# The clustering stage of an attention-and-clustering block: a reordered search, squares on GpSimd, queries projected elsewhere, roots with a bias, and filling in other places

## The chip, the core and the metric

The kernel runs on one core of a Trainium2 chip. The core has a tensor engine (TensorE, PE in the profile, with its weight loads shown apart as PEld), a vector engine (VectorE, DVE), a scalar engine (ScalarE, ACT), a general engine (GpSimd, POOL), and a sync engine (SyncE, SP) that issues most of the transfers. Each engine works through its own list of instructions in order and waits on semaphores for the others. The metric is the time of one execution on the device, in microseconds (us).

## What is computed

The input is four images of 256 channels and 64 x 64 pixels, in float32. Layer 0 is self-attention over the 4096 pixels of an image. Layer 1 normalizes over the whole image, clusters the pixels, projects, and goes through a perceptron and two batch norms. The change touches the clustering and the projections of the next image's attention:

```python
q = einsum('oc,bcn->bno', wq, xf) + bq          # 32 channels
k = einsum('oc,bcn->bon', wk, xf) + bk
attn = softmax(einsum('bnd,bdm->bnm', q, k))
v = einsum('oc,bcn->bon', wv, xf) + bv          # 256 channels
x = gamma[0] * einsum('bcn,bmn->bcm', v, attn) + x
...
feat, val = conv1x1(xn, f_w, f_b), conv1x1(xn, v_w, v_b)   # xn = group_norm(x); 96 channels each
# 4 heads of 24 channels, 2 x 2 folds of the image, 2 x 2 centres in each fold
cn = cen * rsqrt((cen * cen).sum(-1) + 1e-12)
pn = pts * rsqrt((pts * pts).sum(-1) + 1e-12)
sim = sigmoid(beta + alpha * einsum('bmc,bnc->bmn', cn, pn))
mask = one_hot(argmax(sim, axis=1))              # the best of 4 centres for every pixel and head
sim = sim * mask
agg = (einsum('bmn,bnc->bmc', sim, v2) + v_cen) / (mask.sum(-1) + 1.0)
out = einsum('bmn,bmc->bnc', sim, agg)
y = x + ls1 * conv1x1(out, proj_w, proj_b)
```

## The kernel before

The four images go one after the other. For each, `weighting` runs the attention: 8 blocks of 512 queries by 8 groups of 512 keys, 64 units in all. Then `cluster` runs the clustering and `mlp` the perceptron and the pointwise layer. The order of the instructions is written out by hand: an engine does them in the order in which the program emits them, and the text below says "emitted" for that.

**Filling.** Attention of the next image needs its v, its keys and its queries, projected from x. `parts.projections` (L1105) is a list of 36 closures: 32 of `v_half`, each for 128 pixels (two matmuls of 128 x 256 in float32, which the profile counts as four; every second one is followed by a ScalarE copy of a pair, L434), and four of `halved` (keys and queries, each for half of the image: matmuls at L344, a ScalarE op at L361 for the high half, a VectorE op at L362 for the low half, and four transfers to DRAM on SP). `fill(n)` takes the next n of the list and emits them. It is called at many places between the end of `weighting` and the start of the perceptron, where TensorE would wait for a vector chain. Images 0, 1 and 2 have the next image's projections as filling; the last image has `late_block`, the rest of the perceptron of the image before.

**End of `weighting`** (L1061 to L1098). The softmax sums of the last query block are reduced on VectorE (L730, L732), summed over partitions by TensorE (L1070), inverted on VectorE (L1079), sent to all partitions by TensorE (L1085) and copied by ScalarE (L1092). Then the last block is scaled (L1095), added to x (L828) and its statistics taken (`seen`, L832; `pooled`, L837). The block before it is brought back by a transfer that adds to x, `back_one` (L815), issued on GpSimd's queue two units before the end.

**`group_norm`** (L296) makes mean and variance over the whole image with three tiny matmuls (L302, L303, L313), a root on ScalarE and a reciprocal on VectorE (`rsqrt`, L216: add, root, reciprocal). `gn1` is that ahead of the clustering, `gn2` that ahead of the perceptron.

**`cluster`**: centres (`pcen`, L1145), their norms (`len`, L1184), then a loop over 8 pixel blocks (L1281) in which TensorE makes f and v and the products with the centres in one matmul (L1293), VectorE moves them out of PSUM (L1302, L1309), and `heads` squares f (L1273: on GpSimd, for the last block on VectorE) and sums the squares by head (L1274). The image is in two halves, f = 0 (blocks 0 to 3) and f = 1. `similar(f)` (L1227) turns the squares into 1/norm (root and reciprocal), multiplies, and takes tanh on ScalarE; `affine(f)` turns tanh into the sigmoid; `largest(f)` (L1240) finds the best of four centres in five VectorE ops (maximum, is_equal, product with a rank, maximum, is_equal); `weights(f)` masks; `count(f)` counts. `summed` (L1323) then aggregates on TensorE in two passes, first the pooled v, then the weighted v. Counts (L1352), transposes (L1363, L1372), the scaled aggregate (L1376) and its projection `gp` (L1384) follow, and `products` (L1406) spreads the result back over the pixels with the second statistics on VectorE (L1418, L1399). At its end the first three units of the next image's scores are made (`score`, L471; copies at L484; the key loads are issued on SP, L449).

`turn()` makes sums of the perceptron's weights on GpSimd: `turn_mlp` (L246, L247; for the last image it is emitted at L1065 instead) and `turn_w2` (L1577, L1579, L1581). It is emitted after `similar(1)`, so on GpSimd's list it stands right behind the squares of block 6.

The order at the search, whose lines the prediction follows:

```python
        fill(4 if nxt else 2)
        heads(NBLK - 1)
        similar(1)
        fill(0 if nxt else 2)
        summed(lambda j, q: pool_w[:, j], True)
        gelu(1)
        turn()
        fill(8 if nxt else 4)
        table(AF.Sqrt)

        affine(0)
        largest(0)
        affine(1)
        largest(1)
```

Of the kernel before, what the change touches and what calls it, by code (L numbers as in the profile page):

```python
# [14 lines left out]
P = 128  # L15
B, C, H, W = 4, 256, 64, 64
N = H * W
# [43 lines left out]
def attention_then_cluster_block(  # L61
# [153 lines left out]

    def rsqrt(dst, src, eps, meanwhile=lambda: None):  # L216

        nc.vector.tensor_scalar(dst, src, eps, None, ALU.add)
        nc.scalar.activation(dst, dst, AF.Sqrt)
        meanwhile()  # L220
        nc.vector.reciprocal(dst, dst)
# [74 lines left out]
    def group_norm(b, which, stats, fill, between=lambda: None, meanwhile=lambda: None):  # L296
# [19 lines left out]
        fill(3 if which == "gn1" else 2)  # L316
# [14 lines left out]
    def attention(b, xs, ys):  # L331
# [87 lines left out]
        def v_half(i):  # L419
            if i == 0:  # L420
                own["v"] = big.tile([P, N // P, C], F32, tag="v", name=f"v_{b}")
            if i % 2 == 0:
                vps[0] = ps_m.tile([P, 2, C], F32, tag="m", name=f"vp_{b}_{i // 2}")
            o = (i * P) % XT
            for k in range(KC):
                nc.tensor.matmul(  # L426
                    vps[0][:, i % 2, :],
                    xs[i * P // XT][:, k, o : o + P],
                    wv_s[:, k, :],
                    start=(k == 0),  # L430
                    stop=(k == KC - 1),
                )
            if i % 2:
                nc.scalar.copy(own["v"][:, i - 1 : i + 1, :], vps[0])  # L434

        def v_pair(i):
            v_half(2 * i)
            v_half(2 * i + 1)
# [497 lines left out]
        def weighting(next_x, fill, early, begin):  # L936
# [129 lines left out]
            table(AF.Sqrt)  # L1066
            two = ps_s.tile([P, 2, NB], F32, tag="s", name=f"den_{b}_{nb}")
# [9 lines left out]
            fill(2)  # L1077
# [4 lines left out]
            seen(nb - 1)  # L1082
# [10 lines left out]
            fill(6)  # L1093
# [11 lines left out]
        parts.projections = [lambda i=i: v_half(i) for i in range(N // P)]  # L1105
        parts.projections[14:14] = [lambda: halved("q", 0)]
        parts.projections[13:13] = [lambda: halved("k", 0)]
        parts.projections += [lambda: halved("k", 1), lambda: halved("q", 1)]
# [5 lines left out]
    def cluster(b, ys, stats, cells, rest, fill, gelu, nxt, maxima, turn):  # L1114
# [8 lines left out]
        ga, gb = group_norm(b, "gn1", stats, fill, rest, pooling)  # L1123
# [103 lines left out]
        def similar(f):  # L1227

            sg = sgs[f]
            rsqrt(prns[f], prns[f], L2_EPS, lambda: table(AF.Gelu_apprx_tanh))  # L1230
# [9 lines left out]
        def largest(f):  # L1240

            sg, o, best = sgs[f], oh[:, f * 256 : (f + 1) * 256], bests[f]
            nc.vector.tensor_reduce(best, quad(sg), AX.X, ALU.max)
            nc.vector.tensor_tensor(quad(o), quad(sg), over_m(best), ALU.is_equal)
            nc.vector.tensor_tensor(
# [3 lines left out]
            nc.vector.tensor_tensor(quad(o), quad(o), over_m(best), ALU.is_equal)  # L1249

# [858 lines left out]
```

## Time and profile before

The times of three runs are 3134.9, 3135.86 and 3136.3 us; the median is 3135.86 us. The profiled execution took 3135.99 us. Its span, from the first to the last instruction of the program that was recorded, is 3134.2 us. The mean granted clock of TensorE is 0.993.

The clustering stage of image 0, in stretches (times from the start of the span; the columns are microseconds busy on each engine, from the view that sums over windows):

| stretch of image 0 | from - to | length | PE | DVE | ACT | POOL |
|---|---|---|---|---|---|---|
| end of weighting to gn1 | 528.90 - 539.30 | 10.40 | 8.84 | 10.32 | 4.75 | 2.49 |
| gn1 to the first f and v product | 539.30 - 547.90 | 8.60 | 8.47 | 5.95 | 3.18 | 0.00 |
| f and v products | 547.90 - 570.60 | 22.70 | 22.70 | 13.31 | 13.14 | 5.94 |
| to the second aggregation | 570.60 - 584.25 | 13.65 | 13.39 | 10.97 | 6.33 | 6.84 |
| aggregation to the spread | 584.25 - 589.00 | 4.75 | 3.86 | 2.38 | 3.55 | 0.00 |
| spread, statistics, scores, to gn2 | 589.00 - 605.75 | 16.75 | 13.76 | 15.44 | 10.70 | 11.97 |
| gn2 and the start of the perceptron | 605.75 - 613.90 | 8.15 | 6.96 | 5.24 | 4.15 | 3.00 |

The other three images have the same stage from 1299, 2071 and 2818 us on. In the timeline, a row is an instruction (or several alike, "x4"): its start and its duration in us, engine, source line, operation, tile written and tiles read, shape, and in brackets how long the engine was idle before it and what it had been waiting for. A duration runs from when the instruction starts on its engine, so a stand inside it counts as busy. Matmul ends are modelled. In rows of windows the columns are: the window, its length, then busy us and number of instructions of PE, PEld, DVE, ACT and POOL, then the granted TensorE clock, the share of the DMA engines and GB/s.

### The profile page before, as it was taken

How to read it: one execution, taken by the hardware profiler on the slowest of the kernel's cores; microseconds unless marked ns; L12 is line 12 of the kernel's file. 1: busy time of each engine (PE TensorE's matmuls, PEld its weight loads, DVE VectorE, ACT ScalarE, POOL GpSimd, SP SyncE). 2: the span in 40 equal slices, each digit the busy share in tenths (PEclk: the TensorE clock that was granted, in tenths of full speed). 3: DMA queues.
4: the chain of work that ended last, by engine and by line, in shares of the span. 5: the costliest groups of instructions: out<-in, count | busy, mean ns of one | idle time of the engine just before them, and what ended most of it. 6: DMA issues, size and time to landing. Idle time of an engine off the chain costs nothing.

```text
span 3134.2 us, 41370 instructions
## 1 busy us (share of the span) xinstructions
PE 3053.2 (97%) x14210; PEld 2498.2 (80%) x14210; DVE 2514.4 (80%) x3574; ACT 1778.9 (57%) x2817; POOL 2324.7 (74%) x2232
## 2 busy tenths in 40 slices
PE   7999999999999999999999999999999999998999
PEld 5788887788688888878868888886877888875886
DVE  4999888777798888877779888877768988887675
ACT  4666664544566666454456666645446666655344
POOL 5888887477588888647758888955766988893563
PEclk9999999999999999999999999999999999999999
DMA  5112226200112123510011222431011112160000
GB/s 167 45 61 64 61 61 186 71 17 28 48 47 68 55 61 100 154 58 18 28 51 51 65 63 65 113 125 58 28 41 44 59 57 67 54 153 1 14 21 28
DMA packets 105570, 200.40 MB, mean 64 GB/s; under 512 B 14880, under 2 KB 30864, under 8 KB 103824
## 3 DMA queue, kind: packets, MB, share of 16 engines
q1 hardware_dynamic: 100464, 178.66, 18.2%
q0 software_dynamic: 4256, 18.90, 2.9%
q8 instruction: 113, 1.85, 0.2%
q14 instruction: 97, 0.79, 0.1%
q10 hardware_dynamic: 640, 0.20, 0.0%
HBM read 147.01 MB, written 48.34 MB: 62 GB/s over the span
## 4 chain that ended last, share of the span: by engine, by line
PE 74%; DVE 10%; POOL 8%; issue 3%; ACT 3%; DMA 2%; SPq 1%; ACTq 0%; POOLq 0%; DVEq 0%
PE av L716 35%; PE mo L1721 10%; PE sc L471 7%; PE hq L1804 5%; PE hp L1804 3%; PE hr L1804 3%; PE fv L1293 3%; POOL acc L646 2%; DVE top L495 2%; DVE s L637 2%; POOL t L646 2%; POOL s L646 1%; PE mo L1705 1%; DMA w<-in_w 1%; PE vp L426 1%
## 5 line engine op out<-in xcount | busy, mean ns | idle before, releaser
L484 ACT COPY s<-sc 128x1024 f32<-128x1024 f32 x512 | 515.2, 1012 | 433.8 <-PE sc L471 426.3
L637 DVE TENSOR_TENSOR s<-s,hold 128x1024 f32<-128x1024 f32 x512 | 598.6, 1209 | 6.7 <-ACT hold L620 5.0
L646 POOL TENSOR_TENSOR acc<-acc,t 128x512 f32<-128x512 f32 x408 | 541.4, 1347 | 0.0
L716 PE MATMUL av<-s,sum 128*128 128x256 f32 x2048 | 526.9, 380 | 3.7 <-POOL s L646 3.5
L716 PE MATMUL av<-t,v 128*128 128x256 f32 x2048 | 528.0, 380 | 2.5 <-POOL t L646 2.2
L716 PE MATMUL av<-s,v 128*128 128x256 f32 x2048 | 526.7, 380 | 2.1 <-ACT xn L1672 1.1
L646 POOL TENSOR_TENSOR s<-t,s 128x512 f32<-128x512 f32 x256 | 340.5, 1330 | 224.8 <-DVE t L660 157.5
L660 DVE TENSOR_TENSOR t<-s,hold 128x1024 f32<-128x1024 f32 x256 | 311.8, 1218 | 186.6 <-POOL acc L646 95.5
L495 DVE TENSOR_TENSOR top<-sc,top 128x1024 f32<-128x1024 f32 x350 | 426.8, 1219 | 31.4 <-ACT s L484 28.0
L716 PEld LDWEIGHTS av<-s,v 128*128 128x128 f32 x2048 | 387.6, 190 | 64.9 <-ACT xn L1672 2.3
L716 PEld LDWEIGHTS av<-t,v 128*128 128x128 f32 x2048 | 387.9, 190 | 63.2 <-POOL t L646 8.5
L716 PEld LDWEIGHTS av<-s,sum 128*128 128x128 f32 x2048 | 388.1, 190 | 61.3 <-POOL s L646 8.5
L1759 ACT ACTIVATE hs<-hs,pv_s 128x256 f32<-128x256 f32 x496 | 232.5, 502 | 352.6 <-DVE hs L1795 352.6
L471 PE MATMUL sc<-q,k 128*128 128x512 f32 x1024 | 394.2, 469 | 24.8 <-ACT s L484 9.5
L1721 PE MATMUL mo<-hs,w 128*128 128x256 f32 x1512 | 384.8, 381 | 0.0
L646 POOL TENSOR_TENSOR t<-s 128x512 f32<-128x512 f32 x256 | 330.7, 1292 | 46.8 <-PE av L716 33.4
L1721 PEld LDWEIGHTS mo<-hs,w 128*128 128x128 f32 x1512 | 283.8, 190 | 46.8 <-ACT hs L1759 6.2
L641 ACT ACTIVATE hold<-s 128x512 f32<-128x512 f32 x256 | 154.2, 602 | 212.5 <-DVE s L637 210.7
L1795 DVE TENSOR_TENSOR hs<-hq,hs 128x256 f32<-128x256 f32 x496 | 198.7, 421 | 85.9 <-PE hq L1804 75.9
L643 ACT ACTIVATE s<-s 128x1024 f32<-128x1024 f32 x256 | 266.9, 1043 | 0.0
L471 PEld LDWEIGHTS sc<-q,k 128*128 128x128 f32 x1024 | 175.5, 191 | 113.7 <-DVE top L495 54.2
L716 PE MATMUL av<-t,sum 128*128 128x256 f32 x1024 | 262.4, 378 | 0.0
(296 smaller groups left out, 4871.3 us busy)
## 6 DMA issues: line engine op xcount, KB each, us to landing
k<-k SPq DMA_DIRECT2D x248, 256.0 KB, 2.7
x<-in_x SPq DMA_DIRECT2D x62, 512.0 KB, 6.8
out<-xn SPq DMA_DIRECT2D x62, 256.0 KB, 2.1
att<-t SPq DMA_DIRECT2D x56, 256.0 KB, 4.0
x<-att POOLq DMA_DIRECT2D x12, 1024.0 KB, 10.0
w<-in_w SPq DMA_DIRECT2D x8, 1024.0 KB, 12.0
q<-q SPq DMA_DIRECT2D x31, 256.0 KB, 4.0
rden<-row_rd SPq DMA_DIRECT2D x28, 256.0 KB, 3.6
```

Of the source, the lines that this page charges most:

```text
L471: nc.tensor.matmul(sc[:, r, :], k_s[:, (2 * h + r) * P : (2 * h + r + 1) * P], qs[u // GRP], start=True, stop=True,)
L484: nc.scalar.copy(slots[u][:, PAIR[h]].rearrange("p h r n -> p r h n"), tiles(sc))
L495: nc.vector.tensor_tensor(top, src, top if saved[nb] is None else saved[nb], ALU.max)
L637: nc.vector.tensor_tensor(sh, sh, mb.to_broadcast([P, 2, 2, QW]), ALU.subtract)
L643: nc.scalar.activation(s[:, PAIR[1]], s[:, PAIR[1]], AF.Exp)
L646: nc.gpsimd.tensor_tensor(out, x, y, op)
L660: nc.vector.tensor_tensor(t31[u], s[:, B11 : B22 + 1 : 2], b12.to_broadcast([P, 2, 2, QW]), ALU.add)
L716: nc.tensor.matmul(av[bank][:, half_ * QW : (half_ + 1) * QW], a[:, r], t[:, r], start=(g == 0 and r == 0 and i in (1, 7, 2, 4)), stop=(g ...
L1721: return nc.tensor.matmul(bank[:, half * HB : (half + 1) * HB], a[:, j], t, start=start, stop=stop)
L1759: nc.scalar.activation(src, src, AF.Gelu_apprx_tanh, bias=pvc("b1", P, j + 4 * (i > 1)))
L1795: nc.vector.tensor_tensor(dst, ps, term, ALU.add)
L1804: nc.tensor.matmul(out, w, x, start=True, stop=True)
```

## The change

It does six things.

- `rsqrt` leaves out the add on VectorE; the root on ScalarE takes the constant as its bias, from one of three small tiles that GpSimd fills at the start.
- The v projection is split into steps of one matmul (`v_step`, half of `v_half`), and each item of the filling has a size; `fill(n)` takes items until their sizes reach n. The order of the keys within the list moves by one, and the first half of the queries leaves the list.
- Those queries (`parts.queries`) are emitted inside the loop over f and v, after block 2.
- The squares of the last block go to GpSimd like the others. While they run, VectorE gets `affine(0)` and the first op of the search in half 0; while ScalarE takes the root of half 1, the second op. The rest of half 0's search, its weights and its count are emitted ahead of `affine(1)`.
- At the end of `weighting`, one of the two statistics of block 6 is emitted ahead of the reciprocal.
- The filling is spread differently for images 0 to 2: 2 + 1 + 7 at the end of weighting (before 0 + 2 + 6), 2 in gn1 behind the root (before 3), 2 and 5 at the search (before 4 and 8), 0.5 before and 0.5 behind `gp` (before 0 and 0), 3 ahead of the scores (before 1). For the last image it stays as it was.

```diff
+    floors = {}
+    for eps in sorted({BN_EPS, GN_EPS, L2_EPS}):
+        floors[eps] = const.tile([P, 1], F32, name=f"eps{len(floors)}")
+        nc.gpsimd.memset(floors[eps], eps)
+
     def rsqrt(dst, src, eps, meanwhile=lambda: None):
-        nc.vector.tensor_scalar(dst, src, eps, None, ALU.add)
-        nc.scalar.activation(dst, dst, AF.Sqrt)
+        nc.scalar.activation(dst, src, AF.Sqrt, bias=floors[eps])
         meanwhile()
...
-    def group_norm(b, which, stats, fill, between=lambda: None, meanwhile=lambda: None):
+    def group_norm(
+        b, which, stats, fill, between=lambda: None, meanwhile=lambda: None, counts=2
+    ):
...
         rsqrt(rstd, ps2[:, 0:1], GN_EPS, meanwhile)
-        fill(3 if which == "gn1" else 2)
+        fill(counts)
         ga = small.tile([P, KC], F32, tag="ga", name=f"ga_{nm}")
...
-        def v_half(i):
-            if i == 0:
+        def v_step(i, k):
+            if i == k == 0:
                 own["v"] = big.tile([P, N // P, C], F32, tag="v", name=f"v_{b}")
-            if i % 2 == 0:
+            if i % 2 == k == 0:
                 vps[0] = ps_m.tile([P, 2, C], F32, tag="m", name=f"vp_{b}_{i // 2}")
             o = (i * P) % XT
-            for k in range(KC):
-                nc.tensor.matmul(
-                    vps[0][:, i % 2, :],
-                    xs[i * P // XT][:, k, o : o + P],
-                    wv_s[:, k, :],
-                    start=(k == 0),
-                    stop=(k == KC - 1),
-                )
-            if i % 2:
+            nc.tensor.matmul(
+                vps[0][:, i % 2, :],
+                xs[i * P // XT][:, k, o : o + P],
+                wv_s[:, k, :],
+                start=(k == 0),
+                stop=(k == KC - 1),
+            )
+            if i % 2 and k == KC - 1:
                 nc.scalar.copy(own["v"][:, i - 1 : i + 1, :], vps[0])
...
         def v_pair(i):
-            v_half(2 * i)
-            v_half(2 * i + 1)
+            for j in range(2 * i, 2 * i + 2):
+                for k in range(KC):
+                    v_step(j, k)
...
             table(AF.Sqrt)
+            ends = b == B - 1
+            fill(0 if ends else 2)
             two = ps_s.tile([P, 2, NB], F32, tag="s", name=f"den_{b}_{nb}")
...
                 )
-            fill(2)
+            fill(2 if ends else 1)
+            seen(nb - 1, (0,))
             rec = work.tile([P, P], F32, tag="top", bufs=1, name=f"rec_{b}_{nb}")
...
                 pass
-            seen(nb - 1)
+            seen(nb - 1, (1,))
             pooled(nb - 1)
...
             nc.scalar.copy(rdens[nb], inv)
-            fill(6)
+            fill(6 if ends else 7)
             t = ts[nb].rearrange("p (h k) n -> p h k n", h=2)
...
         parts.maximum, parts.first, parts.exps, parts.half = maximum, first, exps, half
-        parts.projections = [lambda i=i: v_half(i) for i in range(N // P)]
-        parts.projections[14:14] = [lambda: halved("q", 0)]
-        parts.projections[13:13] = [lambda: halved("k", 0)]
-        parts.projections += [lambda: halved("k", 1), lambda: halved("q", 1)]
+        parts.projections = [
+            (1 / KC, lambda i=i, k=k: v_step(i, k)) for i in range(N // P) for k in range(KC)
+        ]
+        parts.projections[14 * KC : 14 * KC] = [(1, lambda: halved("k", 0))]
+        parts.projections += [(1, lambda w=w: halved(w, 1)) for w in "kq"]
+        parts.queries = lambda: halved("q", 0)
         return parts
...
-        ga, gb = group_norm(b, "gn1", stats, fill, rest, pooling)
+        ga, gb = group_norm(b, "gn1", stats, fill, rest, pooling, 2 if nxt else 3)
         xns, mix = {}, own_w["mix"]
...
-        def similar(f):
+        def similar(f, between=lambda: None):
+
+            def meanwhile():
+                table(AF.Gelu_apprx_tanh)
+                between()
             sg = sgs[f]
-            rsqrt(prns[f], prns[f], L2_EPS, lambda: table(AF.Gelu_apprx_tanh))
+            rsqrt(prns[f], prns[f], L2_EPS, meanwhile)
             nc.vector.tensor_tensor(quad(sg), quad(sg), over_m(prns[f]), ALU.mult)
...
             nc.vector.tensor_reduce(best, quad(sg), AX.X, ALU.max)
+            yield
             nc.vector.tensor_tensor(quad(o), quad(sg), over_m(best), ALU.is_equal)
+            yield
             nc.vector.tensor_tensor(
...
             nc.vector.tensor_tensor(quad(o), quad(o), over_m(best), ALU.is_equal)
+            yield
...
-        def heads(nb):
+        def heads(nb, between=lambda: None):
...
             f = vf[nb // 2][:, nb % 2, :, :ED]
-            (nc.gpsimd if nb < NBLK - 1 else nc.vector).tensor_tensor(f, f, f, ALU.mult)
+            nc.gpsimd.tensor_tensor(f, f, f, ALU.mult)
+            between()
             nc.vector.tensor_reduce(
...
                 heads(nb - 1)
+            if nxt and nb == 2:
+                nxt.queries()
...
-        fill(4 if nxt else 2)
-        heads(NBLK - 1)
-        similar(1)
+        best = largest(0)
+
+        def ahead():
+            affine(0)
+            next(best)
+
+        fill(2)
+        heads(NBLK - 1, ahead)
+        similar(1, lambda: next(best))
         fill(0 if nxt else 2)
...
         turn()
-        fill(8 if nxt else 4)
+        fill(5 if nxt else 4)
         table(AF.Sqrt)
-
-        affine(0)
-        largest(0)
+        for _ in best:
+            pass
+        weights(0)
+        count(0)
         affine(1)
-        largest(1)
-        weights(0)
+        for _ in largest(1):
+            pass
         weights(1)
         summed(lambda j, q: sim[:, j, q, :], False)
-        count(0)
         count(1)
...
+        fill(0.5 if nxt else 0)
         gp = ps_a.tile([P, NB], F32, tag="a0", name=f"gp_{b}")
...
         nc.scalar.copy(g_s, gp[:, :C])
-        fill(0 if nxt else 1)
+        fill(0.5 if nxt else 1)
         stats2 = small.tile([P, 2 * NBLK, 6], F32, tag="stats", bufs=1, name=f"st2_{b}")
...
         nxt.k_unit(0)
-        fill(1)
+        fill(3)
...
         todo += [lambda c=c, k=k: last(c, k) for c in range(KC) for k in range(KC)]
-        return begin, todo, gelu
+        return begin, [(1, f) for f in todo], gelu
...
         def fill(n):
-            for _ in range(min(n, len(todo))):
-                todo.pop(0)()
+            while n > 0 and todo:
+                size, f = todo.pop(0)
+                n -= size
+                f()
...
```

## Prediction

> **What bounds the kernel now.** I read the page's busy shares first, then the timeline of the clustering stage of the first image engine by engine, then the windows with the granted clock. The busy shares:
>
> ```profile
> PE 3053.2 (97%) x14210; PEld 2498.2 (80%) x14210; DVE 2514.4 (80%) x3574; ACT 1778.9 (57%) x2817; POOL 2324.7 (74%) x2232
> ```
>
> TensorE is idle for 3134.2 - 3053.2 = 81 us, and a good part of it lies in the four clustering stages, which the change edits. There a vector chain sets the end, and "filling" (units of the next image's v projection, about 0.87 us of TensorE each in long rows, 0.95 alone) covers its waits. An edit gains only what it takes out of the idle time, because the filling is conserved. The vector engine's timeline after the f and v products of image 0, which end at 570.68:
>
> ```profile
> 574.19 0.75 DVE L362 SCALAR_TENSOR_TENSOR hl_q<-qp,bqk_s,hl_q 128x512 fp32r<-128x512 f32 x1 [1.79 <-ACT hl_q L361]
> 574.86 1.41 DVE L1273 TENSOR_TENSOR vf<-vf 128x384 f32<-128x384 f32 x1
> 576.30 0.55 DVE L1274 TENSOR_REDUCE prn<-vf 128x16 f32<-128x384 f32 x1
> 576.89 0.56 DVE L218 TENSOR_SCALAR prn<-prn 128x64 f32<-128x64 f32 x1
> ...
> 579.94 0.42 DVE L1245 TENSOR_TENSOR scr<-scr,rank 128x256 f32<-128x256 f32 x1
> ...
> 583.68 0.76 DVE L1253 TENSOR_TENSOR sim<-sg,scr 128x256 f32<-128x256 f32 x2
> ```
>
> The same stretch on GpSimd and TensorE:
>
> ```profile
> 569.62 0.82 POOL L1273 TENSOR_TENSOR vf<-vf 128x384 f32<-128x384 f32 x1 [2.50 <-DVE vf L1302]
> 570.40 1.27 POOL L246 TENSOR_TENSOR w<-w 128x512 f32<-128x512 f32 x1
> 571.77 1.49 POOL L247 TENSOR_SCALAR w<-w 128x512 f32<-128x512 f32 x1
> 573.25 1.25 POOL L1577 TENSOR_TENSOR w<-w 128x512 f32<-128x512 f32 x1
> 574.58 1.28 POOL L1579 TENSOR_TENSOR w<-w 128x512 f32<-128x512 f32 x1
> 575.93 1.47 POOL L1581 TENSOR_TENSOR w<-w 128x512 f32<-128x512 f32 x1
> ...
> 584.25 1.76 PE L1323 MATMUL agg<-vf,sim 128*32 128x96 f32 x64 [0.26 <-DVE sim L1253]
> ```
>
> The chain waits 1.79 us for the queries, then the squares on VectorE take 1.41 us where 128x384 needs about 0.41: they begin at 574.86, GpSimd's L1579 ends at 575.86, and the squares end 0.41 later. L218 (576.89, 0.56) likewise ends with GpSimd's L1581 (577.40). **A VectorE op with two SBUF inputs, or L218's kind, stands until the running GpSimd op is over.** The attention stage has it cleanly:
>
> ```profile
> 173.86 1.34 DVE L552 TENSOR_TENSOR top<-top 128x512 f32<-128x512 f32 x1
> ```
>
> The GpSimd op beside it runs from 173.38 for 1.27 us, to 174.66; 0.55 us later, at 175.21, L552 ends. The weight turning (the five POOL rows above, 6.8 us) is over before the search's tensor ops begin at 578.36, so these run at 0.42 us each.
>
> **The change, part by part** (image 0; images 1 and 2 have the same rows).
>
> *Roots with bias.* The add goes (L218: 0.15 to 0.56 us) and the root takes a bias; a bias costs ScalarE about 0.1 us (128x512: L361 0.69 against L434 0.58). In gn1 the root waited behind 1.2 us of pooling, so 0.1 us is left of it; in gn2 it stands behind a ScalarE copy of v (607.37 to 607.95) and gains nothing; at the start of the kernel the table load moves from 11.14 to about 10.75: -0.4 us once. Three tiny memsets on GpSimd sit in its idle time before 13.2.
>
> *End of weighting.* Statistics of the last block but one (half of them) go before the reciprocal L1079, which starts at 530.88. They read the block that this transfer adds to:
>
> ```profile
> 522.75 1.09 POOL L815 DMA_DIRECT2D x<-att  x1
> ...
> DMA to landing us min/median/max: 6.5/8.9/9.0
> ```
>
> 522.75 + 8.9 = 531.7, so VectorE stands 0.8 us there (image 3: 6.5 us, landed, nothing). Behind it wait the reciprocal and all of VectorE, and for it TensorE's broadcast of 1/den. TensorE: two v units 528.9 to 530.75, den 0.75, one unit 0.95, wait until the reciprocal ends at 532.35 + 0.95 = 533.3, broadcast 0.9, seven units 6.2: 540.4, so gn1's first matmul comes at 540.3 in place of 539.34: +0.95, with two units more done.
>
> *gn1.* `fill(3)` becomes 2: pcen waited for the third unit (it starts 4.23 us after gn1's matmul; the vector chain alone needs 3.7): -0.5. The products start +0.45.
>
> *Queries within f and v.* 16 matmuls, 1.85 us (571.48 to 573.33), in a stage where TensorE has no gap: +1.85, now +2.3. The ScalarE and VectorE ops (0.69, 0.75) fit: they have 1.29 and 1.14 us idle a block. The four writes on SP stand before nothing urgent.
>
> *Search.* Times from the end of the last product. The squares go to GpSimd: they wait for the last `vf` (1.3), 0.83 us, so 2.1. Free of GpSimd the chain would be: affine and maximum by 2.5 (beside the squares), reduce 3.0, root 3.4, is_equal 3.4, reciprocal 3.9, product 4.4, three search ops 5.6, weights 5.9, count 6.4, affine 6.7, five search ops at 0.46, second weights starting at 8.9. Before, they started at 584.02 - 570.68 = 13.3. But the squares now stand **in front of the weight turning** on GpSimd, so its five ops run from 2.1 on, beside exactly these tensor ops. Taking turns as in the rows above, an op of 128x256 ends 0.3 us after the GpSimd op that it met: is_equal 3.8 (L246 ends at 3.5), product 5.3 (L247), rank product 6.6 (L1577), is_equal 7.9 (L1579), weights 9.2 (L1581). GpSimd is then done; count 9.75, affine 10.05, five ops at 0.46, second weights start 12.4. That is 0.9 to 0.95 less than 13.3, not 4.4. The bounds are 8.9 (no meeting) and 13.0 (each op meets a whole one); I take 12.4, as every row with both engines shows the turn-taking. The products' 2.3 less 0.95: **+1.35**.
>
> [...]
>
> *Filling.* Units after the products fall from 4 (one being the queries) + 8 to 2 + 5: TensorE is done 1.85 + 1.45 + 4.45 - 0.16 = 7.6 us after the products and then stands until about 12.6: **5 us idle**, where it had 0.26. Two half units around `gp` cover its waits of 0.47 and 0.46 (+0.1, what they overhang). Two units move into the scoring, where TensorE waits 1.33, 0.17, 0.20 and 0.88 us:
>
> ```profile
> 600.76 0.73 PE L471 MATMUL sc<-q,k 128*128 128x512 f32 x2 [1.33 <-ACT cl L1430]
> ```
>
> They delay the scores' first matmul by 1.9 and, through ScalarE's six copies (0.95 each) and the second key load (2.7 us after the first unit's products), gn2 by 0.3. Per image: 1.35 + 0.1 + 0.3 = **+1.75**.
>
> *The clock.* In image 1 the same scoring waits were followed by half speed:
>
> ```profile
> 1369.00:1373.00 4.00, 2.31 (x9) 0.97 (x7) 4.00 (x8) 3.76 (x6) 3.96 (x4) 0.98 0.04 9
> 1373.00:1383.00 10.00, 9.58 (x25) 7.34 (x26) 6.45 (x19) 5.90 (x8) 5.99 (x5) 0.50 0.18 50
> ```
>
> TensorE was 58% busy over 4 us, and the granted clock was 0.50 for the next 10 us. From the first `op` matmul to the second `hp` this took 24.0 us (1359.38 to 1383.39), in image 0 22.1 (589.04 to 611.14): 1.9 us. Five idle microseconds are worse than these 42%, so I expect half speed behind each search: agg, gp and the first eight `op` matmuls (1.7 + 0.5 + 1.15 = 3.35 us, all on the chain) at nearly double. Bounds 0 and 3.4; the nearest row is 1.9, this stretch has more on the chain, I take 2.5. Image 1's own 1.9 goes, as two units now fill those waits.
>
> [...]
>
> *Last image.* No queries, filling unchanged in number, no late transfer, three turning ops instead of five: by the same turns the second weights start at 10.9, against 10.54 (+0.3).
>
> **Sum**, against the profiled execution, 3135.99 us (span 3134.2; median of the runs 3135.86, so it stands for them): 3 x (1.75 + 2.5) - 0.4 - 1.9 + 0.3 = +10.75, **3146.7 us**. Its own range: search 0.5 a unit either way a image (1.5), clock 1.9 to 3.4 (-1.8, +2.7), late transfer absent (-2), image 1's slow clock staying (+1.9): 3141.5 to 3153.
>
> **Rivals.** *One: the engines do not meet*, because the turning stays out of the way or the pairs of inputs do not collide. Then the search starts 3.5 us earlier, TensorE stands some 1.5 us, the clock holds: 3 x (1.75 - 3.5) - 0.4 - 1.9 - 1.6 (last image, 8.9 against 10.54) = -9.2, 3127. For it: the chain is truly shorter by the 1.79 us wait, the 0.75, the squares and three ops. Against: L1273, L218, L552. It decides if second weights start less than 10.7 us after the products. Chance 0.20.
>
> *Two: they meet, but the clock holds* or its cost hides in VectorE's chain behind `op`: 3 x 1.75 - 0.4 - 1.9 + 0.3 = +3.3, 3139. For it: images 0 and 2 scored with the same waits at full clock. Against: no stretch of 5 idle us like this is in these stages. Chance 0.25.
>
> The forecast has 0.55. A difference under 0.2% (6.3 us) is about what a measurement of this kernel can tell from no change. Rival one is faster by over that (0.20); rival two and the edge of the forecast within it (0.27); the rest slower (0.53). The range is 3127 to 3154, to the middle of rival one and the top of the forecast.
>
> **What would show it.** The five turning ops starting after the eighth squares, and the search's tensor ops at 0.7 to 1.6 us instead of 0.42; 4 to 5 us idle of TensorE before the second `agg`; a granted clock of 0.50 behind it; 0.8 us of VectorE standing at the first L832 before L1079. Wrong if the search ops keep 0.42 us, or if TensorE's wait before `agg` is under 2 us.

## The result and the profile after

The changed kernel takes 3140.88 us (median of 22 runs; before 3134.45, also 22): a ratio of 1.0023, 95% interval 1.0017 to 1.0029, so it is slower by 6.4 us between the medians, 5 to 9 us by the interval. One execution of each kernel (3297.33 and 6381.62 us), and two of experiment 7's eleven (3503.28 and 3932.9), lie far above the rest; they are in the medians and not in the ratios. The prediction had +10.75 us, 3146.7. The profiled execution of the changed kernel took 3139.21 us, with a span of 3137.4. The busy shares on the page of the changed kernel:

```profile
PE 3046.7 (97%) x14210; PEld 2495.5 (80%) x14210; DVE 2512.3 (80%) x3548; ACT 1779.4 (57%) x2817; POOL 2328.2 (74%) x2239
```

TensorE has the same matmuls and 90.7 us without one (3137.4 - 3046.7), where it had 81. The time by stage, read from the start times of the rows in the two timelines, for the f/v products to the end of the last one (us; image 0 / 1 / 2 / 3). `agg` is the aggregation, `op` the product that spreads its result back over the pixels, `hp` the first product of the perceptron:

| stage | before | after |
|---|---|---|
| last `acc<-acc` of VectorE to gn1's first matmul | 15.87 / 15.85 / 15.86 / 16.61 | 17.00 / 16.87 / 17.00 / 16.27 |
| to the first f/v product | 8.57 / 8.57 / 8.57 / 9.30 | 8.01 / 8.00 / 8.00 / 7.52 |
| f/v products | 22.77 in each | 24.82 / 24.82 / 24.82 / 22.67 |
| search, to the second masked weights | 13.33 / 13.33 / 13.48 / 10.53 | 11.66 / 11.53 / 11.67 / 10.84 |
| to the first `op` matmul | 5.03 / 5.03 / 5.03 / 5.36 | 6.23 / 6.49 / 7.09 / 6.83 |
| to gn2's first matmul | 16.71 / 17.04 / 16.71 / 16.80 | 16.71 / 16.71 / 17.04 / 16.80 |
| to the second `hp` matmul | 5.38 / 6.97 / 5.36 / 10.22 | 5.40 / 5.39 / 6.09 / 10.22 |
| sum | 87.67 / 89.56 / 87.79 / 91.60 | 89.83 / 89.82 / 91.72 / 91.14 |

The four sums differ by +2.16, +0.26, +3.93 and -0.46: +5.9 us. Between these stages the kernels agree within 0.4 us an image, and behind the last the one after is 0.8 us shorter; ahead of image 0's it is 2.7 us shorter, as the profile before has half clock at 38, 55 and 240 us and this one has not. So the two profiled executions differ by 3.2 us, not by 5.9. The search of image 0 in the changed kernel, VectorE's timeline (start, length, engine, line, operation, tiles; the eighth block's products end at 570.58):

```profile
574.71 0.43 DVE L1246 TENSOR_TENSOR sg<-sg,prn 128x256 f32<-128x256 f32 x1
575.06 0.42 DVE L1262 TENSOR_TENSOR scr<-scr,rank 128x256 f32<-128x256 f32 x1
...
575.96 1.14 DVE L1266 TENSOR_TENSOR scr<-scr 128x256 f32<-128x256 f32 x1
577.14 1.37 DVE L1271 TENSOR_TENSOR sim<-sg,scr 128x256 f32<-128x256 f32 x1
578.43 0.57 DVE L1279 TENSOR_REDUCE scr<-scr 128x32 f32<-128x256 f32 x1
578.92 1.00 DVE L1253 TENSOR_SCALAR sg<-sg 128x256 f32<-128x256 f32 x1
579.96 0.42 DVE L1258 TENSOR_REDUCE scr<-sg 128x64 f32<-128x256 f32 x1
...
582.24 0.42 DVE L1271 TENSOR_TENSOR sim<-sg,scr 128x256 f32<-128x256 f32 x1
```

GpSimd in the same stretch, the eighth squares (L1291) and the five turning ops:

```profile
571.82 0.83 POOL L1291 TENSOR_TENSOR vf<-vf 128x384 f32<-128x384 f32 x1 [1.99 <-DVE vf L1321]
572.60 1.33 POOL L250 TENSOR_TENSOR w<-w 128x512 f32<-128x512 f32 x1
574.03 1.54 POOL L251 TENSOR_SCALAR w<-w 128x512 f32<-128x512 f32 x1
575.55 1.26 POOL L1605 TENSOR_TENSOR w<-w 128x512 f32<-128x512 f32 x1
576.90 1.33 POOL L1607 TENSOR_TENSOR w<-w 128x512 f32<-128x512 f32 x1
578.31 1.33 POOL L1609 TENSOR_TENSOR w<-w 128x512 f32<-128x512 f32 x1
```

L1266 ends at 577.10, 0.29 us after L1605 (576.81); L1271 and L1253 end 0.28 after L1607 and L1609. But L1246 and L1262 fall inside L251, the one op with a single tensor input, and take their 0.42 us. TensorE waits for the second weights, 0.38 and 3.71 us, and half clock follows (its timeline, then the windows with busy times and, third from the end, the granted clock):

```profile
578.66 0.36 PE L1344 MATMUL agg<-vf,sim 128*32 128x96 f32 x4 [0.38 <-DVE sim L1271]
582.72 1.84 PE L1344 MATMUL agg<-vf,sim 128*32 128x96 f32 x60 [3.71 <-DVE sim L1271]
584.50 0.58 PE L1379 MATMUL cnt<-scr,ones 128*96 128x64 f32 x2
```

```profile
583.76:587.17 3.41, 3.41 (x32) 3.08 (x25) 1.21 (x4) 0.96 (x3) 0.00 (x0) 0.50 0.00 0
```

At the end of the weighting VectorE stands at the statistics that were moved ahead of the reciprocal (L1088):

```profile
529.10 0.69 DVE L838 BATCH_NORM_STATS2 st<-x 128x6 f32<-128x512 f32 x1 [0.84 <-DMA x<-att]
529.71 0.94 DVE L1088 RECIPROCAL rec<-den 128x128 f32<-128x128 f32 x1
```

### The profile page after: what moved, and what is told of

It reads as the page before. It is cut to its first block, busy times and chain, and to the rows that moved or that the text cites. A ratio compares the mean times of both kernels' runs of the same rounds, so it can differ in the third digit from the quotient of the medians.

```text
span 3137.4 us, 41354 instructions
## 1 busy us (share of the span) xinstructions
PE 3046.7 (97%) x14210; PEld 2495.5 (80%) x14210; DVE 2512.3 (80%) x3548; ACT 1779.4 (57%) x2817; POOL 2328.2 (74%) x2239
## 3 DMA queue, kind: packets, MB, share of 16 engines
q8 instruction: 113, 1.85, 0.2%
## 4 chain that ended last, share of the span: by engine, by line
PE 74%; DVE 9%; POOL 8%; issue 3%; ACT 3%; DMA 3%; SPq 0%; ACTq 0%; POOLq 0%; DVEq 0%
PE av L722 34%; PE mo L1749 10%; PE sc L477 7%; PE hq L1832 5%; PE hp L1832 3%; PE hr L1832 3%; PE fv L1312 3%; POOL acc L652 2%; PE vp L431 2%; DVE top L501 2%; POOL t L652 2%; POOL s L652 2%; DVE s L643 1%; PE mo L1733 1%; ACT s L490 1%
## 6 DMA issues: line engine op xcount, KB each, us to landing
w<-in_w SPq DMA_DIRECT2D x8, 1024.0 KB, 11.5
```

## The experiments

Theory: the meeting of VectorE's search with GpSimd's turning, the queries in the f/v loop, the wait for the late transfer and the half clock each cost what the stage shows, and they add. Rivals stand in each expectation. Ratios are to the kernel before, with 95% intervals.

**1. The turning out of the search's way.** `turn()` becomes a generator, and one step follows each of the squares of blocks 2 to 6:

```diff
+            if nb > 2:
+                next(turning, None)
...
         gelu(1)
-        turn()
```

> The changed kernel with the five weight-turning ops of GpSimd moved ahead: one behind each of the squares of blocks 2 to 6 of the f/v loop, where GpSimd stands some 2 us a block. Theory (the search is slow because GpSimd's tensor ops stand beside it): all search ops fall to 0.42 us, the second weights start 8.9 us behind the products in place of 11.65, TensorE's wait ahead of the second agg falls from 4.1 to about 1.4 us, and with it the half clock behind the search goes in most images. Per image -2.7 and -1.2 to -1.5, last image -1.9: some 14 us below the changed kernel (which stands 6.5 above before), so about -8 us against before. Rival one (the chain itself is 11 us long, the two engines' meeting is worth little): within 2 us of the changed kernel, +4.5 to +7. Rival two (the meeting is only moved: the f/v loop's own VectorE ops stand beside the turning): the f/v loop grows by 1 us or more an image.

Measured: 3129.35 us, 0.9985 (0.9977 to 0.9994), 11.5 us below the changed kernel where 14 were expected. The second weights start at 9.42 us in all four images; VectorE's and TensorE's timelines of this kernel (products end at 573.23):

```profile
578.74 0.42 DVE L1269 TENSOR_TENSOR scr<-scr 128x256 f32<-128x256 f32 x1
579.20 0.43 DVE L1274 TENSOR_TENSOR sim<-sg,scr 128x256 f32<-128x256 f32 x1
579.55 0.58 DVE L1282 TENSOR_REDUCE scr<-scr 128x32 f32<-128x256 f32 x1
580.04 0.28 DVE L1256 TENSOR_SCALAR sg<-sg 128x256 f32<-128x256 f32 x1
```

```profile
583.13 1.51 PE L1352 MATMUL agg<-vf,sim 128*32 128x96 f32 x60 [1.91 <-DVE sim L1274]
```

The same ops that took 1.14, 1.37 and 1.00 us take 0.42, 0.43 and 0.28. The f/v loop stays at 24.82: of its VectorE ops, those that move f and v out of PSUM (PSUM and one SBUF tile) take 0.56 us also inside a turning op. One op of the loop has two SBUF inputs, the product of half 0 (L1249), and it does stand: from 570.08 for 1.10 us, until 0.29 us behind the turning op L1615 (569.62 to 570.89). VectorE has idle time there, so it costs TensorE nothing. Rivals one and two fall. The chain was 0.5 us longer than the 8.9 expected; its first affine op (574.86) still took 0.72 us, as the eighth squares on GpSimd run until 575.29. And half clock still came behind the search in images 1 and 2 (+1.2 us each).

**2. The statistics back behind the reciprocal.**

```diff
-            seen(nb - 1, (0,))
...
-            seen(nb - 1, (1,))
+            seen(nb - 1)
```

> The changed kernel with both statistics of the last block but one behind the reciprocal of the denominators, as before. Theory (VectorE waits for the late transfer ahead of the reciprocal, TensorE for the reciprocal): TensorE's wait of 1.16 us ahead of the broadcast of 1/den falls below 0.3, the stage from the last accumulation to gn1's first matmul falls from 17.0 to about 16.0 in images 0 to 2: 2.5 to 3.4 us below the changed kernel, about +3.5 against before. Rival (the stage is longer because two more units of filling stand in it): it stays at 16.9 to 17.0 and the time at +6.5.

Measured: the stage falls to 16.28, 16.25 and 16.24 us, TensorE does not wait ahead of the broadcast, gn1 is 0.1 longer. So 0.6 to 0.8 us an image come back, not 1.0; the 0.4 that stay above the kernel before stand with the filling that was added here, which no run takes out alone. The time, 1.0015 (1.0007 to 1.0024), cannot be told from the changed kernel's: 2 us are less than two such intervals show, and the 2.5 to 3.4 us that were expected are not seen.

**3. More filling in the search.**

```diff
-            fill(6 if ends else 7)
+            fill(6)
...
-        fill(5 if nxt else 4)
+        fill(8 if nxt else 4)
...
-        fill(3)
+        fill(1)
```

> The changed kernel with eight units of filling in the search in place of five (one taken from the end of the weighting, two from the scoring). Theory (the idle time ahead of the second agg brings half clock behind it, worth 1.2, 1.5 and 2.1 us in images 0 to 2): the wait falls from 4.1 to about 1.4 us, no record of half clock behind the search, the stretch from the second agg to the first op matmul back to 5.0 us in each image: 4 to 5 us below the changed kernel, about +2 against before, less whatever the scoring's bare waits cost again (0 to 1.9 in one image). Rival (VectorE's chain hides the half clock, or the clock falls anyway): +6 to +7 against before.

Measured: 3139.8 us, 1.0015 (1.0006 to 1.0024), so 1 us below the changed kernel and not 4 to 5. The clock part came out: no half clock behind any of the four searches, and from the second weights to the first `op` matmul 5.03 us in images 0 to 2, as before. But the search grew to 12.78:

```profile
569.12 1.92 PE L350 MATMUL kp<-x,wqk_s 128*32 128x512 f32 x16
...
576.82 4.58 PE L431 MATMUL vp<-wv_s,x 128*128 128x256 f32 x20 [0.47 <-ACT v L439]
581.34 0.36 PE L1344 MATMUL agg<-vf,sim 128*32 128x96 f32 x4
582.45 1.51 PE L1344 MATMUL agg<-vf,sim 128*32 128x96 f32 x60 [0.76 <-DVE sim L1271]
```

The list of filling is consumed in order, so one unit less ahead moved the keys (1.92 us) from gn1, which fell to 7.08, into the search. And the bare scoring brought half clock from 600.3 to 610.6 in image 0 (a mean granted clock of 0.68 from 595 to 611; 6.94 us to the second `hp`, where it had been 5.40). The clock's price is shown; this balance gives it back elsewhere.

**4. The queries out of the f/v loop**, with their matmuls behind the five units and VectorE's half behind the last count:

```diff
-            if nxt and nb == 2:
-                nxt.queries()
...
         fill(5 if nxt else 4)
+        late_q = nxt.queries() if nxt else iter(())
+        next(late_q, None)
...
         count(1)
+        next(late_q, None)
```

> The changed kernel with the queries out of the f/v loop: their matmuls and ScalarE's half behind the five units in the search, where TensorE waits 4.1 us, and VectorE's half behind the last count, off the chain. Theory (the queries cost their 16 matmuls where TensorE has no gap, and nothing where it waits): the f/v loop falls from 24.8 to 22.8 us, the search stays at 11.7, TensorE's wait ahead of the second agg falls to 2.2 us: -6 us from the loop and 0 to -4 from the clock, so +0.5 to -3.5 us against before. Rival (a filling unit moved is a unit moved, and the loop's gain comes back as a later score because the queries reach memory 24 us later): the time within 2 us of the changed kernel, with a longer wait of TensorE ahead of the first scores.

Measured: 3134.66 us, 0.9998 (0.9989 to 1.0007). The f/v loop is 22.77 in images 0 to 2 (-2.05 each, 6.15 in all, and the median is 6.2 lower); the search stays at 11.5 to 11.7, and the scores are made no later. Half clock still follows each search, as TensorE waited 2.46 us:

```profile
577.56 1.92 PE L350 MATMUL qp<-x,wqk_s 128*32 128x512 f32 x16
579.30 0.34 PE L1355 MATMUL agg<-vf,sim 128*32 128x96 f32 x4
582.10 2.78 PE L1355 MATMUL agg<-vf,sim 128*32 128x96 f32 x60 [2.46 <-DVE sim L1284]
```

**5. The negation as a two-input op.**

```diff
-        nc.gpsimd.tensor_scalar(w_d, w_d, -1.0, None, ALU.mult)
+        nc.gpsimd.tensor_tensor(w_d, w_d, w_cd, ALU.subtract)
```

> The changed kernel with the one GpSimd op of the turning that has a single tensor input (the negation, 1.5 us) made a subtraction of two tensors, at the same place and size; the turned weights and so everything behind them have other values. Theory (VectorE's ops with two SBUF inputs stand beside a two-input GpSimd op, and did not stand beside the negation): the product of similarity and root (0.43 us now) and the one by rank stand until 0.3 us behind a GpSimd op, and the second weights start about 12.4 us behind the products in place of 11.65, as the prediction had it. Rival (they ran at 0.42 because they happened to fall between GpSimd's accesses, whatever its op): 11.5 to 11.8 as now.

Measured (one run, 3146.82 us): the second weights start at 12.28 us in images 0 to 2. The two ops that ran free now stand, as VectorE's and GpSimd's timelines show:

```profile
577.73 0.91 DVE L1246 TENSOR_TENSOR sg<-sg,prn 128x256 f32<-128x256 f32 x1
578.57 1.49 DVE L1262 TENSOR_TENSOR scr<-scr,rank 128x256 f32<-128x256 f32 x1
```

```profile
577.03 1.33 POOL L251 TENSOR_TENSOR w<-w 128x512 f32<-128x512 f32 x1
578.32 1.45 POOL L1605 TENSOR_TENSOR w<-w 128x512 f32<-128x512 f32 x1
```

L1246 ends at 578.64, 0.28 after L251; L1262 at 580.06, 0.29 after L1605. The rival falls. The two forms differ in the number of tensor inputs and in the operation (tensor_scalar, tensor_tensor); which of the two counts, these runs do not separate.

**6. All five turning ops with one input.** The four other ops become multiplications of one tensor by -1, as the negation is.

> The changed kernel with all five turning ops of GpSimd made multiplications of one tensor by -1, at the same place and of the same size; the turned weights and all behind them have other values. Theory: GpSimd is busy for 7 us beside the search as now, but nothing stands: the search ops take 0.42 us each and the second weights start at 9.4 us, as with the turning moved ahead. Open within it: whether VectorE's affine ops (one tensor input, 0.58 and 1.00 us now, 0.28 alone) still stand. Rival (any GpSimd op beside them slows VectorE): 11 to 11.7 us.

Measured (one run, 3130.42 us): second weights at 9.97 to 9.98 us in images 0 to 2. GpSimd is busy from 574.94 to 582.53 without a gap, and the search beside it:

```profile
577.03 0.42 DVE L1246 TENSOR_TENSOR sg<-sg,prn 128x256 f32<-128x256 f32 x1
...
578.28 0.51 DVE L1266 TENSOR_TENSOR scr<-scr 128x256 f32<-128x256 f32 x1
...
579.66 0.56 DVE L1253 TENSOR_SCALAR sg<-sg 128x256 f32<-128x256 f32 x1
...
581.17 0.75 DVE L1262 TENSOR_TENSOR scr<-scr,rank 128x256 f32<-128x256 f32 x1
```

Most ops are free; the three longest lose 0.1 to 0.3 us, and L1253 and L1262 start within 0.2 us of a GpSimd op's start (579.47, 581.04). It is nearly, not wholly, free of standing: 0.5 us in the search instead of 2.2.

**7. The kernel before with the turning moved alone.** The same generator, in the kernel before.

> The kernel before with only the turning moved into the f/v loop, one op behind each of the squares of blocks 2 to 6; nothing of the change itself. Theory (in the kernel before TensorE is the bound of the search, eight units of filling with 0.26 us idle ahead of the second agg, so a shorter VectorE chain gains nothing that TensorE does not let through): the last squares fall from 1.41 to 0.42 us and the add of the root from 0.56 to 0.15, yet the stage falls only from 13.3 to about 13.0 in images 0 to 2, and by up to 1 us in the last: -1 to -2 us in all. Rival (the chain's 1.4 us come out in full): -4 to -6 us.

Measured: 3130.51 us, 0.9984 (0.9975 to 0.9994), as far as the rival said, but not for its reason. The squares take 0.55 us and the root's add 0.20; the second weights start at 12.11 (-1.2), but the second agg is now held by TensorE's own units (no wait ahead of it) and ends only 0.7 us earlier, 14.66 behind the products in place of 15.32. Three times 0.7 and the last image's search (9.57 in place of 10.53) make 3 us; 3.3 more are half clock that this profile does not have in image 1 (6.97 to 5.38) and in image 3's gn1 (9.30 to 7.60). Whether those two go because of the edit or with the position of the clock's intervals stays open.

**8. The three corrections together** (1, 2 and 4).

> The changed kernel with the turning in the f/v loop, the queries behind the five units in the search (VectorE's half of them behind the last count), and both late statistics behind the reciprocal. Theory (the terms add, as each sits in another stage): against the run with the turning moved alone (-5 against before) -2.05 an image from the f/v loop, -0.6 an image from the end of the weighting, and no half clock behind the search, as the queries' 1.9 us fill the 1.9 us that TensorE still waited: -13 to -16 us against before, 3118 to 3121 us. Rival (the stages are coupled: the queries now end behind the second weights, or the scoring's waits bring the half clock there): -8 to -11 us.

Measured: 3119.55 us, 0.9948 (0.9934 to 0.9962). The stages are those of the parts: 16.26, 8.11, 22.77, 9.42, and 5.03 behind the search in images 0 to 2, with no half clock there. TensorE's timeline:

```profile
578.97 1.92 PE L352 MATMUL qp<-x,wqk_s 128*32 128x512 f32 x16
580.71 0.34 PE L1362 MATMUL agg<-vf,sim 128*32 128x96 f32 x4
581.23 1.51 PE L1362 MATMUL agg<-vf,sim 128*32 128x96 f32 x60 [0.19 <-DVE sim L1286]
```

**9. The squares of the last block back on VectorE.**

```diff
-            nc.gpsimd.tensor_tensor(f, f, f, ALU.mult)
+            (nc.gpsimd if nb < NBLK - 1 else nc.vector).tensor_tensor(f, f, f, ALU.mult)
```

> The changed kernel with only the squares of the eighth block back on VectorE, so that GpSimd's turning starts at the end of the seventh block's squares, some 2 us earlier. Theory (what the squares' move did was to push the turning onto the search; a two-input VectorE op stands until 0.3 us behind a two-input GpSimd op and runs free beside the negation): the squares run at 0.42 us beside the negation, the first search ops still meet three turning ops, which are over at 5.5 us behind the products in place of 8.6; second weights at 9.6 to 10.2 us in place of 11.65, so -1.5 to -2 an image, -1 to -1.5 more from the clock in the images whose wait of TensorE ahead of the second agg falls under 2.5 us: -1 to +2 us against before. Rival (the squares meet a whole op themselves, as the 1.41 us in the kernel before, and all behind them shifts): 11.5 to 12.5 us, +6 or more.

Measured: 3139.77 us, 1.0014 (1.0005 to 1.0024); second weights at 11.08, between theory and rival. The squares took 0.55 us beside the negation, as long as in experiment 7 (0.42 was expected), but the first affine op stood 1.37 us beside L1605, which the expectation had not counted (VectorE's row, then GpSimd's):

```profile
574.38 1.37 DVE L1253 TENSOR_SCALAR sg<-sg 128x256 f32<-128x256 f32 x1
```

```profile
574.33 1.27 POOL L1605 TENSOR_TENSOR w<-w 128x512 f32<-128x512 f32 x1
```

So the squares' move costs 0.6 us an image while the turning stands behind them; what counts is the turning's place.

**10. The keys moved like the queries**, on top of 8, with the first count behind the second weights and half units between the scores (the `for` line stands in `queries()`):

```diff
-        parts.projections[14 * KC : 14 * KC] = [(1, lambda: halved("k", 0))]
+            for w in "kq":
...
-        fill(5 if nxt else 4)
+        fill(4)
...
-        count(0)
         affine(1)
...
+        count(0)
         count(1)
...
+            if u < 2:
+                fill(0.5)
```

> The best kernel so far (turning in the f/v loop, queries behind the search's filling, statistics back: 3119.6 us) with the keys moved like the queries (matmuls behind the search's filling, one unit less there, VectorE's halves behind the counts and behind the sum's scaling), the first count behind the second weights, and two half units between the scores. Theory (a move gains where it takes TensorE's work out of a place without a gap and puts it into a wait): gn1 to the f/v loop -0.8 us an image, the search +0.1 in images 0 to 2 and -0.46 in the last, the half units within the scoring's waits of 0.65 and 0.63 us: -2 to -3 us against the best, 3116.5 to 3117.5 us. Rival (VectorE, not TensorE, sets the stretch from gn1 to the f/v loop, and two halves on VectorE delay the counts): 3119 to 3121 us.

Measured: 3135.4 us, 1.0000 (0.9991 to 1.0009), a miss by 18 to 19 us. gn1 fell to 7.08 and the second weights start at 8.93, as the first count's 0.5 us are behind them now. But the queries waited for the keys, and from the second weights to the first `op` it took 8.57 us in place of 5.03; the second half's keys fell into gn2, and gn2 to the second `hp` took 8.56 in place of 5.4:

```profile
578.45 1.92 PE L352 MATMUL qp<-x,wqk_s 128*32 128x512 f32 x16 [1.89 <-DVE hl_k L375]
```

**11. An even number of units ahead of them.** One edit against 10: `fill(3 if nxt else 4)` in place of `fill(4)`.

> The kernel with the keys moved too, with three units in place of four behind the pooled sum in the search. Theory (in the run before this one the queries' matmuls waited 1.89 us for VectorE's half of the keys, because 21 units leave a pair of v half done: it holds one of the two PSUM buffers, the keys the other; and the list of filling ran out one unit too early, so that the second half's keys fell into gn2): with 20 units no pair is open, the queries follow the keys without a wait, the second agg ends 11.4 us behind the products as in the best kernel so far (3119.6 us), gn2 to the second hp is back at 5.4, and gn1 to the f/v loop keeps its -1.0 us an image and the last image its -0.5: 3115.5 to 3117 us, -18 to -20 against before. Rival (the queries wait for the keys for another reason, the tiles of the halves or the order on VectorE): the wait of 1.9 us stays and with it 3124 us or more.

Measured: 3116.32 us, 0.9938 (0.9924 to 0.9951), the best of all, 19 us below before. The wait is gone, from the second weights to the first `op` it takes 5.42 us, and gn2 to the second `hp` is 5.2. v pairs, keys and queries share two PSUM buffers (`ps_m`). The queries now start at 579.74, ahead of VectorE's half of the keys (582.08), so with no pair open a buffer is free for them:

```profile
577.99 1.92 PE L352 MATMUL kp<-x,wqk_s 128*32 128x512 f32 x16 [0.20 <-ACT v L461]
579.74 1.90 PE L352 MATMUL qp<-x,wqk_s 128*32 128x512 f32 x16
581.45 1.50 PE L1368 MATMUL agg<-vf,sim 128*32 128x96 f32 x64
```

## Why the prediction was right, and where its sizes were off

The direction came out, and the mechanisms of the main terms. Two of these terms were put too dear, the term at the start of the kernel had the wrong sign, and the other differences cancel. The time alone would not have decided: 3140.88 us lies 0.6 us under the forecast's own range (3141.5 to 3153) and nearer to rival two's 3139 than to 3146.7. The rows decide.

- **End of weighting** +0.95: measured +1.13, +1.02, +1.14, with VectorE standing 0.84 us where 0.8 was said. Experiment 2 gives 0.6 to 0.8 of it to the late transfer.
- **gn1** -0.5: measured -0.56. **Queries within f and v** +1.85: measured +2.05, and experiment 4 gets exactly that back. TensorE has no gap there, so its matmuls cost their full length (554.39 to 556.25), 1.86 us; of the 2.05 that leaves 0.1 us for the change of kind at either end, an estimate.
- **Search** -0.95 to -0.9: measured -1.67 to -1.81 (second weights at 11.6, not 12.4). This is the step that was mis-sized. It let an op stand at each of the five turning ops, L247 (now L251) among them. Rows L1246 and L1262 show that this one did not hold them up, and experiment 5, which makes it a two-input op, lands at 12.28. That "every row with both engines shows the turn-taking" was too much: in the last image of the kernel before, a VectorE op with two SBUF inputs (0.41 us in image 0) runs beside L247. It takes twice its time, yet ends 0.6 us ahead of L247's end:

```profile
2820.80 1.81 POOL L247 TENSOR_SCALAR w<-w 128x512 f32<-128x512 f32 x1
...
2821.18 0.83 DVE L762 TENSOR_TENSOR t<-t,t 128x256 f32<-128x256 f32 x1
```

Without any meeting with the turning the second weights start at 9.42 (experiment 1), where the bound said 8.9. The 0.41 us given for squares of 128x384 on VectorE are 0.55 in experiments 7 and 9; the sum does not use them.
- **Clock** 2.5 an image: half clock came behind each search as forecast, and cost 1.20, 1.46 and 2.06 us (5.03 to 6.23, 6.49, 7.09), and 1.47 in the last image, where the prediction had none. Mis-sized because the step let nearly all work up to the eighth `op` matmul run at half speed; the records show one interval of 3.41 us (two in image 2) at a granted clock of 0.50, in each of which at most half, 1.7 us, can be lost. Five idle microseconds were not needed for it: waits of 4.1 us (image 0) and 2.3 us (image 3) were followed by it too.
- **Filling around `gp`** +0.1: nothing, since the stretch is 5.03 us in experiments 3 and 8 as before.
- **Roots with bias**: the 128x64 root takes 0.31 to 0.35 us in place of 0.26, the 0.1 that was said. The -0.4 at the start had the wrong sign. ScalarE's table loads there, in the kernel before and in the changed one:

```profile
2.09 1.28 ACT L219 ACT_TABLE_LOAD   x1 [2.09 <-issue]
...
11.14 1.28 ACT L294 ACT_TABLE_LOAD   x1
```

```profile
10.28 1.28 ACT L223 ACT_TABLE_LOAD   x1 [10.28 <-DMA pc_s<-in_pc]
...
12.07 1.28 ACT L298 ACT_TABLE_LOAD   x1
```

Before, VectorE's add waited for the transfer of the constants (until 10.22 us) while ScalarE had long loaded the root's table (from 2.09). With the bias the root reads the constants itself, its table load stands behind the transfer, and the next load comes 0.93 us later, not 0.4 earlier. The first copy of v (13.48 in place of 12.55) and the first scores (26.22 in place of 25.29) come later by as much.
- **Scores and gn2** +0.3: measured 0, -0.3 and +0.3 up to gn2, where the two changes are the clock's, so nothing at full clock. Image 1's half clock went as forecast (17.04 to 16.71 and 6.97 to 5.39 us, 1.9 in all), but image 2 took 1.1 us of such a loss itself (0.3 and 0.7).
- **Last image** +0.3 in the search: +0.31. Its total is -0.46, since gn1's half clock of the profile before (1.8 us) is absent.

The search's 0.8 and the clock's 0.9 an image are 5 us, as much as lies between the forecast's +10.75 and the +5.9 of the stages. That the other differences cancel (the last image's two clock changes, +1.5 and -1.8 us, image 2's +1.1, the queries, the start) is luck, and so is that +5.9 comes near the 6.4 of the medians: the changed kernel's profile has a mean clock of 0.996, its 21 compared runs 0.993. Runs of equal mean clock, 0.992 to 0.995, lie 4.2 to 4.9 us above those of the kernel before. Its mean is 0.9932, against 0.9943 over the 76 runs of the kernel before that stand beside experiments, and 0.001 is worth 1.3 us within either kernel; so more half clock makes some 1.5 us of the difference, an estimate, where the forecast had 5.6 net (3 x 2.5 - 1.9).

Rival one fell by its own point of decision (11.5 to 11.7 us, not under 10.7); experiment 1, which takes the meeting away, comes to 3129.35 us, near the 3127 that this rival was given. Rival two fell with the half clock behind the search in every image of the profile, and by that alone.

The prediction's rule, that a VectorE op with two SBUF inputs stands until the running GpSimd op is over, holds for the two-input ops of GpSimd here (0.28 to 0.29 us behind their ends) and overstates it for the one-input op: 0.42 us within L251, and 0.83 us, not blocked to its end, beside the same op in the last image before.

## What to carry to other kernels

An op moved to another engine moves the whole queue behind it: the squares' 0.83 us on GpSimd were cheap, the five ops that then met VectorE's search were not. Put such a queue where its neighbours read PSUM (0.56 us inside a turning op as outside one, experiment 1), and take TensorE's work out of places without a gap into places where it waits; the two moves were worth 11 and 6 us, and with the waits filled the clock held too behind the searches of images 0 to 2 (experiment 8). When an item of a shared list of filling moves, look at what it displaces: once the keys landed in the search, once a half-done pair held the buffer that the next product needed. And where a root takes its constant as a bias, ask what its engine now waits for: here the table load came to stand behind a transfer.

## What the hardware showed unexpectedly

- The GpSimd op with one tensor input (a tensor_scalar in every case here) let VectorE's two-input ops run: 0.43 and 0.42 us inside 1.54 us of L251, and 0.91 and 1.49 us when the same place held a two-input op. It was not always free: 0.75 in place of 0.42 us in experiment 6, 0.83 in place of 0.41 in the last image before. VectorE ops that read PSUM and SBUF did not stand beside two-input GpSimd ops (0.56 us in experiment 1's loop); VectorE's affine op, one SBUF input, did (1.00 and 1.37 us, 0.28 alone), and its reduction, one SBUF input too, did not (L1265, 0.42 us at 575.51 beside L1605).
- The granted clock fell to 0.50 in intervals of 3.41 us or whole multiples (6.83, 10.24 and 13.65 in the records of the kernel before). In the changed kernel those behind the searches start at 583.76, 1355.17, 2126.58 and 2874.10 us, and the last three lie 226, 452 and 671 times 3.4133 us behind the first. There a single one cost 1.2 to 1.5 us and two in a row 2.1 (image 2); in experiments 1 and 9 one cost 1.2. The compared runs of the changed kernel spread from 3134.61 us (mean clock 0.997) to 3146.91 (0.989), twice the difference between the two kernels.
- With a wait of TensorE of 1.91 us ahead of the second agg the clock held in image 0 and fell in images 1 and 2 (experiment 1); with 0.19 it held in images 0 to 2 (experiment 8). TensorE's busy time just ahead does not decide it alone: in the 3.41 us before the changed kernel's intervals behind the searches it was busy 1.04, 0.01, 0.92 and 1.26 us, but in the kernel before 2.08 us from 598.03 were followed by full clock and 2.08 us from 2826.93 by half. That the same wait falls into one stretch of 3.41 us or is split by two would fit the spacing above; it is the author's estimate, and no run shows it.
